# Delta rule on keys and queries as the convolution leaves them: their norms and beta scale rows of the system, the right side and the outputs

## The chip, the cores and the metric

The kernel runs on one core of one Trainium2 chip. The metric is the device time of a run in microseconds (us). The kernel before took 1627.59 us, the median of 3 runs (1624.23 to 1631.69). Beside the timed runs there is one profiled execution, from which every duration below comes.

## The reference, cut to what matters

The program is two layers on 4 sequences ("batches") of 512 tokens with 512 channels. Each layer adds attention times the SiLU of a feed-forward net to its input. The change concerns the attention of the second layer, a gated delta rule with 6 heads of 64:

```
q = silu(causal_conv(x @ Wq.T, conv_q));  k, v likewise
q = q * rsqrt(sum(q*q) + 1e-6);  k = k * rsqrt(sum(k*k) + 1e-6)     # per token and head
beta = sigmoid(x @ Wb.T);  g = -exp(A_log) * softplus(x @ Wa.T + dt_bias)
per token:  S = S * exp(g)
            u = beta * (v - k.S)
            S = S + outer(k, u)
            o = (q * 64**-0.5).S
o = o * rsqrt(mean(o*o) + 1e-5) * o_norm_w * silu(x @ Wg.T);  out = o @ Wo.T
```

The first layer has a softmax attention with 32 heads, and a feed-forward net with Hadamard transforms. The feed-forward net of the second layer multiplies with the signs of its weights.

## The kernel before, in words

Layer 0 fills the first 837 us. One loop over u runs the softmax attention two heads at a time (scores L402, maxima L403, second scores L423, exponentials L425, values L435), and 16 steps behind it the feed-forward net (L316 up and gate, L334 down). In the first batch of it the weights are folded with the Hadamard matrix as they are needed (`mix`, `fold`, loads of `raw`). The same loop also prepares the second layer: `load_weights` and `signs` read each of 32 blocks of the sign weights into a tile `sn` of three buffers, take the sign on ACT (L498) and store it to `sgn_d`. `sn` lies in the pool `zp`, which opens where the pool of the folded weights (`a0`) closes.

Layer 1 works on one batch b after the other, in tiles t of 128 tokens, four a batch.

- *Projections.* `project` (n = 0 to 8: three blocks of 128 channels each of q, k and v) makes one block with the channels on the partitions, convolves it on DVE (L719) and applies SiLU (L723, L724). `to_tokens(b, n, t)` turns three blocks of one tile to tokens on the partitions with three PE transposes (L736), copies them to `z` on ACT (L737), squares them on POOL (L740) and sums the squares per head on DVE (L741). `gate1` makes the output gate and, with its last block, beta and the decays. `norms` turns the sums into 1/norm.
- *Head products.* `scale_heads` on POOL scales k by its norm (L918), makes kb = beta k (L920), scales q (L921), and makes kd and vb (L923, L925). `to_heads` turns kn, kb and qn back to channels on the partitions: nine PE transposes a tile (L933) and three copies on ACT (L935). `tile_decays` makes the decay matrix of a tile (POOL gm L941, PE L943, ACT L945, POOL dT L946). `head_products` multiplies k with kb (A) and with qn (W) (L956), evacuates them times the decays on DVE (L961), and stores the 32x32 diagonal blocks of A to memory.
- *Solve.* `solve_load` reads the 32x32 blocks of the four tiles, one block a partition; 31 `solve_step`s of two DVE operations each (L989, L993) invert them; `solve_store` writes the result, `load_UT` reads it back per tile. In the last batch this is done in two halves of two tiles.
- *Chunk chain.* Per tile `blocks32` to `blocks64b` build the inverse of the 128x128 system from the blocks (products L1020, L1046, evacuated with a factor -1 on ACT, L1023 and L1049), `with_state`, `new_values`, `state` and `outputs` carry the state S through the tiles. `out_norms`, `gated`, `project_out` and `project_out2` end a tile; for all but the last batch they run with the head products of the next.

The calls are put into one list of steps with weights (`add`); while it is emitted, the pieces of the second feed-forward net (`up1` L878, `down1` L891) are strewn in by weight, so that PE has other work. The solve of batch b is strewn among the projections of batch b + 1. A scheduler then orders each engine's instructions by when it thinks that they are ready. All loads and stores after the setup are issued by SP, in order. PSUM gives layer 1's attention three banks (`bank`).

Of the kernel before, what the change touches and what calls it, by code (L numbers as in the profile page):

```python
# [18 lines left out]
P = 128  # L19
# [14 lines left out]
def kernel(ctx: ExitStack, tc: tile.TileContext, i: dict, out: bass.AP):  # L34
# [68 lines left out]
    if True:  # L103
# [383 lines left out]
        def load_weights(n):  # L487
            c, m = n // 2, n % 2
            sg = sns[n] = new(zp[0], [P, DM], F32, "sn", bufs=3)
            if m == 0:  # L490
                nc.sync.dma_start(
                    sg.rearrange("p (k n) -> p k n", k=KC), i["upT"][:, ts(c, P)].rearrange("(k p) n -> p k n", p=P)
                )
            else:
                nc.sync.dma_start(sg, i["downT"][ts(c, P), :])
# [92 lines left out]
    UT_d = new(dram, [NB, TB, NH, 4, 2, 32, 32], F32, "UT_d")  # L588
    gate_d = new(dram, [NB, VC, P, TB, P], F32, "gate_d")


# [45 lines left out]
    for name in ("conv_q", "conv_k", "conv_v"):  # L637
# [15 lines left out]
                            pattern=[[-1, P]], channel_multiplier=1)  # L653

    st = [{} for _ in range(NB)]

    def decays(b):
# [31 lines left out]
    def decay_sums(b):  # L689

        s = st[b]
        small = [P, TB, NH]
        pcum = bank()
        gf = s["g"].rearrange("p t h -> p (t h)")
        for n, m in enumerate((le, gt, ones)):
            nc.tensor.matmul(pcum[:, ts(n, TB * NH)], m, gf, start=True, stop=True)
        ex = s["ex"] = new(ce, [P, 3, TB, NH], F32, "ex", bufs=2)
        nc.scalar.activation(ex.rearrange("p n t h -> p (n t h)"), pcum[:, : 3 * TB * NH], AF.Exp)
        beG = s["beG"] = new(ce, small, F32, "beG", bufs=2)
        nc.vector.tensor_tensor(beG, s["beta"], ex[:, 0], ALU.mult)  # L700
        hb = s["hb"] = new(ce, small, F32, "hb", bufs=2)
        nc.vector.tensor_scalar(hb, s["beta"], 0.5, None, ALU.mult)

        etp = s["etp"] = new(ce, [P, TB, VC], F32, "etp", bufs=2)
        et = ex[:, 2].rearrange("p t (m u) -> p t m u", u=2)
        for u in range(2):
            nc.vector.tensor_copy(etp[64 * u : 64 * u + 64], et[64 * u : 64 * u + 64, :, :, u])

    def project(b, n):

        s = st[b]
        pp = bank()
        for k in range(KC):
            nc.tensor.matmul(pp, wps[b, n][:, k, 0:P], xn1Ts[b][:, k, :], start=(k == 0), stop=(k == KC - 1))  # L714
        w = convs[n // VC][:, n % VC, :]
        yc = new(ce, [P, SEQ], F32, "yc", bufs=4)
        nc.scalar.activation(yc, pp, AF.Copy, scale=w[:, 3:4])
        for d in range(1, 4):
            nc.vector.scalar_tensor_tensor(  # L719
                yc[:, d:], pp[:, : SEQ - d], w[:, 3 - d : 4 - d], yc[:, d:], ALU.mult, ALU.add  # L720
            )
        th = new(ce, [P, SEQ], F32, "cth")
        nc.scalar.activation(th, yc, AF.Tanh, scale=0.5)  # L723
        nc.vector.scalar_tensor_tensor(yc, th, 1.0, yc, ALU.add, ALU.mult)  # L724
        s["yc", n] = yc

    def to_tokens(b, n, t):
        s = st[b]
        if n == 0 and t == 0:
            s["ss"] = new(ce, [P, TB, 2, NH], F32, "ss", bufs=2)  # L730
        if t == 0:
            s["z", n] = new(ce, [P, TB, VD], F32, f"z{n}")
        zt = s["z", n][:, t, :]
        pz = bank()
        for m in range(VC):
            nc.tensor.transpose(pz[:, ts(m, P)], s["yc", VC * n + m][:, ts(t, P)], identf)  # L736
        nc.scalar.copy(zt, pz[:, :VD])  # L737
        if n < 2:
            sq = new(ce, [P, VD], F32, "sq")
            nc.gpsimd.tensor_tensor(sq, zt, zt, ALU.mult)  # L740
            nc.vector.tensor_reduce(s["ss"][:, t, n, :], v6(sq), AX.X, ALU.add)  # L741

# [20 lines left out]
    def norms(b):  # L763
        ss = st[b]["ss"]
        nc.vector.tensor_scalar(ss, ss, 4e-6, None, ALU.add)
        nc.scalar.activation(ss, ss, AF.Sqrt)
        nc.vector.reciprocal(ss, ss)
        nc.vector.tensor_scalar(ss[:, :, 0, :], ss[:, :, 0, :], HD**-0.5, None, ALU.mult)

# [6 lines left out]
    def projections(b, between=()):  # L776
# [16 lines left out]
        for n in range(9):  # L793
# [3 lines left out]
            if n == 1:  # L797
                add(0.3, decay_sums, b)
            if n % 3 == 0 and n:
                for t in range(TB):  # L800
                    add(0.34, to_tokens, b, n // 3 - 1, t)
                    some()
        for m in range(VC - 1):
            prefetch()
            add(3.6, gate1, b, m)
            some()
            if m == 0:
                for t in range(TB):
                    add(0.34, to_tokens, b, 2, t)
                    some()  # L810
                add(0.0, norms, b)
# [10 lines left out]
    cm = ctx.enter_context(tc.tile_pool(name="cm", bufs=1, side="left"))  # L822
    c0 = ctx.enter_context(tc.tile_pool(name="c0", bufs=1, side="left"))
    d0 = ctx.enter_context(tc.tile_pool(name="d0", bufs=2, side="right"))
    dps = ctx.enter_context(tc.tile_pool(name="dps", bufs=1, space=PSUM))
# [88 lines left out]
    def scale_heads(b, t):  # L914
        s = st[b]
        ss = s["ss"]
        qn, kn = s["z", 0][:, t, :], s["z", 1][:, t, :]
        nc.gpsimd.tensor_tensor(v6(kn), v6(kn), bc_in(ss[:, t, 1, :], HD), ALU.mult)  # L918
        kb = s["kb", t] = new(c0, [P, VD], F32, "kb")
        nc.gpsimd.tensor_tensor(v6(kb), v6(kn), bc_in(s["beta"][:, t, :], HD), ALU.mult)  # L920
        nc.gpsimd.tensor_tensor(v6(qn), v6(qn), bc_in(ss[:, t, 0, :], HD), ALU.mult)  # L921
        kd = s["kd", t] = new(c0, [P, VD], F32, "kd", bufs=TB)
        nc.gpsimd.tensor_tensor(v6(kd), v6(kn), bc_in(s["ex"][:, 1, t, :], HD), ALU.mult)  # L923
        vb = s["vb", t] = new(c0, [P, VD], F32, "vb", bufs=TB)
        nc.gpsimd.tensor_tensor(v6(vb), v6(s["z", 2][:, t, :]), bc_in(s["hb"][:, t, :], HD), ALU.mult)  # L925

    def to_heads(b, t):
        s = st[b]
        qn, kn = s["z", 0][:, t, :], s["z", 1][:, t, :]
        for src, tag, n in ((kn, "knT", TB), (s["kb", t], "kbT", 1), (qn, "qnT", TB)):  # L930
            pz = bank()
            for m in range(VC):
                nc.tensor.transpose(pz[:, ts(m, P)], src[:, ts(m, P)], identf)  # L933
            s[tag, t] = new(c0, [P, VC, P], F32, tag, bufs=n)
            nc.scalar.copy(s[tag, t], v3(pz))  # L935

# [11 lines left out]
    def head_products(b, t, right, tag):  # L948
# [4 lines left out]
        for m in range(3):  # L953
            for u in range(2):
                rows = ds(64 * u, 64)
                ins = nc.tensor.matmul(ps[u][:, ts(m, P)], s["knT", t][rows, m, :], s[right, t][rows, m, :],  # L956
                                       start=True, stop=True)
                if m + u > 0:
# [13 lines left out]
    def solve_load(b, t0=0, nt=TB):  # L972
# [3 lines left out]
        Ab = s["Ab"] = new(c0, [P, 32, 32], F32, "Ab")  # L976
        nc.sync.dma_start(Ab[:NBL].rearrange("p r c -> p (r c)"), A_d[b, t0 : t0 + nt].rearrange("t h k r c -> (t h k) (r c)"))
        UT = s["UT"] = new(c0, [P, 2, 32, 32], F32, "UT")
        nc.gpsimd.memset(UT[:, 0], 0.0)
        nc.gpsimd.memset(UT[:, 0].rearrange("p r c -> p (r c)")[:, 0 : 32 * 32 : 33], 1.0)  # L980

    def solve_step(b, j):
# [9 lines left out]
        )  # L992
        nc.vector.tensor_tensor(U[:, 0 : j + 1, j + 1 :], U[:, 0 : j + 1, j + 1 :], x, ALU.subtract)  # L993

# [18 lines left out]
    def blocks32(b, t):  # L1013
# [8 lines left out]
        X = s["X32"] = new(c0, [P, NH, 32], F32, "X32")  # L1022
        nc.scalar.activation(X, px[:, : NH * 32].rearrange("p (h n) -> p h n", h=NH), AF.Copy, scale=-1.0)  # L1023

# [16 lines left out]
    def blocks64(b, t):  # L1041
# [6 lines left out]
        X = s["X64"] = new(c0, [P, NH, 64], F32, "X64")  # L1048
        nc.scalar.activation(X[64:128], v6(px)[64:128], AF.Copy, scale=-1.0)  # L1049

# [10 lines left out]
    def with_state(b, t):  # L1061
# [10 lines left out]
        for m in range(VC):  # L1072
            nc.tensor.matmul(pks[:, ts(m, P)], s["knT", t][:, m, :], S[:, m, :], start=True, stop=True)
        R = s["R"] = new(c0, [P, VD], F32, "R")
# [3 lines left out]
        for m in range(VC):  # L1078
            nc.tensor.matmul(pqs[:, ts(m, P)], s["qnT", t][:, m, :], S[:, m, :], start=True, stop=True)
        tq = s["tq"] = new(c0, [P, VD], F32, "tq")  # L1080
# [41 lines left out]
    def out_norms(b, t=None):  # L1122
        so = st[b]["so"] if t is None else st[b]["so"][:, t]
        nc.vector.tensor_scalar(so, so, 1.0 / HD, EPS, ALU.mult, ALU.add)
        nc.scalar.activation(so, so, AF.Sqrt)
        nc.vector.reciprocal(so, so)

    def gated(b, t):
# [37 lines left out]
    for b in range(NB):  # L1166
# [10 lines left out]
        for t in range(TB):  # L1177
# [5 lines left out]
            for u in range(2):  # L1183
                add(0.7, tile_decays, b, t, u)
                if t >= 2:
                    some(2)
            add(1.1, to_heads, b, t)
            add(0.8, head_products, b, t, "kbT", "A")
            if t >= 2:
                some(3)  # L1190
            if b > 0 and not last:
                add(0.4, project_out, b - 1, t)
            add(0.8, head_products, b, t, "qnT", "W")
            if t >= 2:
# [113 lines left out]
```

## Time and profile before

| what | value |
|---|---|
| median of the runs | 1627.59 us |
| the profiled execution: its time, its span | 1629.15 us, 1627.2 us |
| mean granted TensorE clock | 0.967 |
| layer 0, then layer 1 | 0 to 837 us, 837 to 1627 us |
| head products of batches 0, 1, 2 | 912 to 936.5, 1075 to 1128, 1266 to 1318 us |
| projections of batches 1, 2, 3 | 936.5 to 1011, 1128 to 1200, 1318 to 1392 us |
| critical chain by engine | PE 59%, DVE 22%, DMA 7%, POOL 4%, ACT 4%, issue 3% |

The times of the profile are those of one execution. "Busy" counts an engine's instructions, not how well they use it. Matmuls overlap, so their listed duration is a latency; how long PE is taken by one is read from the starts of two that follow each other. A wait is put down to the operation that came last. The granted clock is 1.00 where TensorE runs at full speed.

### The profile page before, as it was taken

What the parts mean: (1) busy time and instruction counts of PE and PEld (TensorE: products, weight loads), DVE (VectorE), ACT (ScalarE), POOL (GpSimd) and SP (SyncE); (2) the same over time, 40 slices, a digit from 0 to 9 for tenths busy, and PEclk for the clock granted to TensorE, in tenths of its full rate; (3) what the DMA queues carried; (4) which work ended last, traced back from release to release, by engine and by line L of the source; (5) the groups of instructions that cost most, each with busy time, mean ns of one, the idle gap of its engine ahead of it and who ended that gap; (6) DMA issues with size and microseconds to landing.
All of it is one profiled execution on the core that took longest, in us unless ns stands there. A gap on an engine that the chain in (4) does not pass through costs nothing.

```text
span 1627.2 us, 23201 instructions
## 1 busy us (share of the span) xinstructions
PE 1509.9 (93%) x8284; PEld 904.0 (56%) x8284; DVE 1007.8 (62%) x1799; ACT 680.1 (42%) x1007; POOL 419.7 (26%) x424
## 2 busy tenths in 40 slices
PE   6999988999999999999998999989999999999767
PEld 2556432555335543465344666866578666776555
DVE  6899544665556655665437487464946469547754
ACT  4655555666446654565424433132332323222013
POOL 1111100322013210222013713162232713244014
PEclk9999999999999999999998999999999999999779
DMA  7855446665116520363035333344344343333413
GB/s 274 327 192 191 146 151 185 224 219 167 26 45 232 202 75 22 119 225 122 18 89 163 102 105 103 95 143 135 87 128 124 102 125 98 95 98 84 116 45 107
DMA packets 191955, 215.85 MB, mean 133 GB/s; under 512 B 66016, under 2 KB 128864, under 8 KB 190944
## 3 DMA queue, kind: packets, MB, share of 16 engines
q1 hardware_dynamic: 189088, 213.23, 41.5%
q8 instruction: 66, 1.08, 0.3%
q10 hardware_dynamic: 2752, 1.14, 0.3%
q14 instruction: 49, 0.40, 0.1%
HBM read 155.18 MB, written 54.53 MB: 129 GB/s over the span
## 4 chain that ended last, share of the span: by engine, by line
PE 59%; DVE 22%; DMA 7%; POOL 4%; ACT 4%; issue 3%; SPq 1%; POOLq 0%; ACTq 0%; DVEq 0%
PE y L334 13%; PE mm L316 10%; PE ph L878 5%; PE y L891 4%; DVE yc L719 4%; PE sc L402 3%; DVE sx L989 3%; DVE UT L993 3%; PE po L435 2%; DVE nmx L403 2%; PE pu L753 2%; PE mm L243 2%; PE pu L1157 2%; PE pu L1088 1%; PE pu L956 1%
## 5 line engine op out<-in xcount | busy, mean ns | idle before, releaser
L403 DVE TENSOR_REDUCE nmx<-sc 128x2 f32<-128x1024 f32 x256 | 312.2, 1220 | 156.8 <-PE st L423 129.6
L425 ACT ACTIVATE pe<-st 128x1024 f16<-128x1024 f32 x256 | 262.8, 1026 | 145.1 <-PE st L423 143.7
L334 PE MATMUL y<-wdn,hT 128*128 128x512 f32 x512 | 258.7, 626 | 4.7 <-DVE g L338 3.8
L316 PE MATMUL mm<-xr,wc 128*128 128x512 f32 x768 | 209.4, 414 | 0.4 <-DVE th L323 0.4
L327 POOL TENSOR_TENSOR hT<-hT,th 128x512 f32<-128x512 f32 x64 | 83.4, 1303 | 323.3 <-ACT hT L326 249.2
L316 PEld LDWEIGHTS mm<-xr,wc 128*128 128x128 f32 x768 | 138.6, 191 | 49.5 <-issue 21.9
L334 PEld LDWEIGHTS y<-wdn,hT 128*128 128x128 f32 x512 | 87.3, 191 | 93.6 <-issue 85.7
L714 PE MATMUL pu<-xn1T,wp 128*128 128x512 f32 x288 | 129.7, 595 | 0.7 <-DVE yc L719 0.5
L452 POOL TENSOR_TENSOR oT<-os,sm 128x512 f16<-128x512 f32 x32 | 41.4, 1293 | 322.7 <-DMA sm<-rec_d 295.7
L878 PE MATMUL ph<-xsh,sg 128*128 128x512 f32 x256 | 114.4, 447 | 4.3 <-ACT hT L883 2.3
L423 PE MATMUL st<-qm,kT 32*128 32x512 f16 x512 | 102.7, 387 | 9.5 <-ACT pe L425 9.4
L402 PE MATMUL sc<-kT,qT 32*128 32x512 f16 x512 | 102.8, 386 | 8.4 <-DVE nmx L403 8.1
L878 PE MATMUL ph<-xsl,sg 128*128 128x512 f32 x256 | 106.0, 414 | 0.0
L891 PE MATMUL y<-sg,hsh 128*128 128x512 f32 x256 | 90.9, 455 | 4.9 <-DVE hsh L853 3.9
L883 ACT ACTIVATE hT<-ph,upsc 128x512 f32<-128x512 f32 x64 | 44.0, 687 | 111.7 <-PE ph L878 100.9
L714 PEld LDWEIGHTS pu<-xn1T,wp 128*128 128x128 f32 x288 | 53.7, 190 | 57.0 <-issue 53.1
L323 DVE SCALAR_TENSOR_TENSOR th<-th,mm 128x512 f32<-128x512 f32 x64 | 43.6, 682 | 65.5 <-ACT th L322 65.3
L402 PEld LDWEIGHTS <-qT 32*128 32x128 f16 x512 | 26.1, 91 | 101.1 <-issue 94.6
L853 DVE CAST hsh<-hT 128x512 fp32r<-128x512 f32 x64 | 32.4, 507 | 79.3 <-ACT hT L883 79.2
L891 PE MATMUL y<-sg,hsl 128*128 128x512 f32 x256 | 76.5, 412 | 0.0
L316 PE MATMUL mm<-xr,fo 128*128 128x512 f32 x256 | 72.3, 421 | 0.0
L322 ACT ACTIVATE th<-mm,hwg 128x512 f32<-128x512 f32 x64 | 44.0, 688 | 58.9 <-PE mm L316 58.9
(277 smaller groups left out, 2577.9 us busy)
## 6 DMA issues: line engine op xcount, KB each, us to landing
wc<-wS SPq DMA_DIRECT2D x96, 512.0 KB
sg<-sgn_d SPq DMA_DIRECT2D x128, 256.0 KB
wS<-fo SPq DMA_DIRECT2D x16, 1024.0 KB
sm<-rec_d SPq DMA_DIRECT2D x128, 64.0 KB
sgn_d<-sn SPq DMA_DIRECT2D x32, 256.0 KB
raw<-in_w_gateT SPq DMA_DIRECT2D x8, 512.0 KB
hT<-in_w_downT SPq DMA_DIRECT2D x16, 256.0 KB
raw<-in_w_upT SPq DMA_DIRECT2D x8, 512.0 KB
```

Of the source, the lines that this page charges most:

```text
L316: nc.tensor.matmul(pgs[m], wcs[b, c, m][:, h, k, :], xrs[b][:, k, :], start=(k + h == 0), stop=(k == KC - 1 and h == 1))
L327: nc.gpsimd.tensor_tensor(hT, hT, ths[b, c], ALU.mult)
L334: nc.tensor.matmul(ys[t], hTs[b, c][:, ts(t, P)], wdn[:, c, :], start=(c == 0), stop=(c == NI - 1))
L402: nc.tensor.matmul(sc[:, j, :], qTs[n][rows, ts(t, P)], kTs[b, g // 4][rows, :], start=True, stop=True)
L403: nc.vector.tensor_reduce(nmxs[n][:, t, 2 * pr : 2 * pr + 2], sc, AX.X, ALU.max, negate=True)
L423: nc.tensor.matmul(st[:, j, :], kTs[b, g // 4][rows, ts(k, P)], qms[n][rows, :], start=True, stop=True)
L425: nc.scalar.activation(pes[u], st, AF.Exp)
L714: nc.tensor.matmul(pp, wps[b, n][:, k, 0:P], xn1Ts[b][:, k, :], start=(k == 0), stop=(k == KC - 1))
L719: nc.vector.scalar_tensor_tensor(yc[:, d:], pp[:, : SEQ - d], w[:, 3 - d : 4 - d], yc[:, d:], ALU.mult, ALU.add)
L878: ins = nc.tensor.matmul(ph, sgs[b, c, 0][:, ts(k, P)], xss[b][n][:, k, :], start=(k + n == 0), stop=(k == KC - 1 and n == 1))
L891: ins = nc.tensor.matmul(yss[b][t], hss[b, c][n][:, ts(t, P)], sgs[b, c, 1], start=(c + n == 0), stop=(c == NI - 1 and n == 1))
L989: nc.vector.tensor_tensor(x, Ab[:, j, j + 1 :].unsqueeze(1).to_broadcast([NBL, j + 1, r]), U[:, 0 : j + 1, j : j + 1].to_broadcast([NBL, j ...
```

## The change

`scale_heads` no longer scales q and k, kb is gone, and `to_heads` is removed with its transposes. The products, and the products with the state, read the convolution's own output `yc`, which has the channels on the partitions. For that the six blocks of q and k keep a buffer each, in one of two pools by the batch's parity; v's blocks share two. What the norms and beta did is put elsewhere: the rows of the 32x32 blocks are multiplied by c = beta / |k|^2 after their load (DVE; c goes through memory to come to the blocks' partitions), the two evacuations X32 and X64 multiply by -c in place of -1 and so move from ACT to DVE, the right side takes beG and hb with the norms in them, and the output norm takes the q norm in. `to_tokens` is called once per block of channels: four transposes, for q only a square on ACT from PSUM (no z), for k a copy and a square of 512 columns. `norms` computes c and its relatives, transposes -c on PE, and stores it. The sign tiles `sn` move from pool `zp` to pool `b0`.

```diff
-            sg = sns[n] = new(zp[0], [P, DM], F32, "sn", bufs=3)
+            sg = sns[n] = new(b0, [P, DM], F32, "sn", bufs=3)
...
-        yc = new(ce, [P, SEQ], F32, "yc", bufs=4)
+        if n < 2 * VC:
+            yc = new(home[b % 2], [P, SEQ], F32, f"yc{n}")
+        else:
+            yc = new(ce, [P, SEQ], F32, "yv", bufs=2)
...
+    def to_tokens(b, n):
...
+        for t in range(TB):
+            nc.tensor.transpose(pz[:, ts(t, P)], s["yc", n][:, ts(t, P)], identf)
...
+        sq = new(ce, [P, TB, P], F32, "sq")
+        if kind == 0:
+            nc.scalar.activation(sq, pz, AF.Square)
+        else:
+            zt = s["z", 1][:, :, ts(m, P)]
+            nc.scalar.copy(zt, pz)
             nc.gpsimd.tensor_tensor(sq, zt, zt, ALU.mult)
...
     def norms(b):
...
-        nc.vector.tensor_scalar(ss[:, :, 0, :], ss[:, :, 0, :], HD**-0.5, None, ALU.mult)
+        rq = s["rq"] = new(ce, small, F32, "rq", bufs=2)
+        nc.vector.tensor_scalar(rq, ss[:, 0], HD**-0.5, None, ALU.mult)
+        hb = s["hb"] = new(ce, small, F32, "hb", bufs=2)
+        nc.vector.tensor_tensor(hb, s["beta"], ss[:, 1], ALU.mult)
+        c = new(ce, small, F32, "c")
+        nc.vector.tensor_tensor(c, hb, ss[:, 1], ALU.mult)
+        nc.vector.tensor_scalar(hb, hb, 0.5, None, ALU.mult)
+        beG = s["beG"] = new(ce, small, F32, "beG", bufs=2)
+        nc.vector.tensor_tensor(beG, c, s["ex"][:, 0], ALU.mult)
+        ng = s["negc"] = new(ce, small, F32, "negc", bufs=2)
+        for u in range(2):
+            nc.vector.tensor_scalar(
+                ng[:, :, 3 * u : 3 * u + 3], c.rearrange("p t (m u) -> p t u m", u=2)[:, :, u], -1.0, None, ALU.mult
+            )
+        pz = bank()
+        nc.tensor.transpose(pz[: TB * NH, 0:P], ng.rearrange("p t h -> p (t h)"), identf)
+        cr = new(ce, [P, TB, P], F32, "sq")[: TB * NH, 0, :]
+        nc.vector.tensor_copy(cr, pz[: TB * NH, 0:P])
+        nc.sync.dma_start(c_d[b], cr)
...
     def scale_heads(b, t):
-        nc.gpsimd.tensor_tensor(v6(kn), v6(kn), bc_in(ss[:, t, 1, :], HD), ALU.mult)
-        kb = s["kb", t] = new(c0, [P, VD], F32, "kb")
-        nc.gpsimd.tensor_tensor(v6(kb), v6(kn), bc_in(s["beta"][:, t, :], HD), ALU.mult)
-        nc.gpsimd.tensor_tensor(v6(qn), v6(qn), bc_in(ss[:, t, 0, :], HD), ALU.mult)
...
-    def to_heads(b, t):
...
-                ins = nc.tensor.matmul(ps[u][:, ts(m, P)], s["knT", t][rows, m, :], s[right, t][rows, m, :],
-                                       start=True, stop=True)
+                ins = nc.tensor.matmul(ps[u][:, ts(m, P)], s["yc", VC + m][rows, ts(t, P)],
+                                       s["yc", right + m][rows, ts(t, P)], start=True, stop=True)
...
+        cb = new(c0, [P, 32], F32, "cb")
+        nc.sync.dma_start(cb[:NBL], c_d[b, ds(t0 * NH, nt * NH)].rearrange("h (k r) -> (h k) r", r=32))
+        nc.vector.tensor_tensor(Ab[:NBL], Ab[:NBL], bc_mid(cb[:NBL], 32), ALU.mult)
...
-        nc.vector.tensor_tensor(U[:, 0 : j + 1, j + 1 :], U[:, 0 : j + 1, j + 1 :], x, ALU.subtract)
+        nc.vector.tensor_tensor(U[:, 0 : j + 1, j + 1 :], U[:, 0 : j + 1, j + 1 :], x, ALU.add)
...
-        nc.scalar.activation(X, px[:, : NH * 32].rearrange("p (h n) -> p h n", h=NH), AF.Copy, scale=-1.0)
+        nc.vector.tensor_tensor(
+            X, px[:, : NH * 32].rearrange("p (h n) -> p h n", h=NH), bc_in(s["negc"][:, t, :], 32), ALU.mult
+        )
...
-        nc.scalar.activation(X[64:128], v6(px)[64:128], AF.Copy, scale=-1.0)
+        nc.vector.tensor_tensor(X[64:128], v6(px)[64:128], bc_in(s["negc"][64:128, t, :], HD), ALU.mult)
...
     def out_norms(b, t=None):
...
+        for _ in range(2):
+            nc.vector.tensor_tensor(so, so, rq, ALU.mult)
...
+        nc.vector.tensor_tensor(so, so, rq, ALU.mult)
...
-            add(1.1, to_heads, b, t)
-            add(0.8, head_products, b, t, "kbT", "A")
+            add(0.8, head_products, b, t, VC, "A")
```

## The prediction

> **What bounds the kernel now.** I read the page first, then the critical chain, then cut the second half into its stages with the table of stretches. The page's first part says which engine is full:
>
> ```profile
> PE 1509.9 (93%) x8284; PEld 904.0 (56%) x8284; DVE 1007.8 (62%) x1799; ACT 680.1 (42%) x1007; POOL 419.7 (26%) x424
> ```
>
> TensorE is the bound on average, but the stages differ. Six of them (columns: stretch, length, then busy us and count for PE, PEld, DVE, ACT, POOL, then granted clock, DMA share, GB/s):
>
> ```profile
> 912.00:936.50 24.50, 23.36 (x168) 16.05 (x166) 9.99 (x18) 10.45 (x23) 17.19 (x20) 1.00 0.41 116
> 936.50:1011.00 74.50, 70.80 (x304) 47.52 (x304) 62.91 (x155) 25.23 (x45) 21.96 (x23) 0.98 0.38 108
> 1011.00:1075.00 64.00, 64.00 (x626) 53.31 (x625) 33.72 (x61) 13.62 (x24) 15.24 (x16) 1.00 0.36 103
> 1453.50:1482.90 29.40, 24.95 (x147) 17.77 (x145) 10.57 (x19) 9.88 (x21) 22.64 (x26) 0.88 0.21 51
> 1482.90:1524.20 41.30, 33.87 (x134) 21.16 (x132) 35.42 (x79) 6.11 (x12) 10.63 (x10) 0.92 0.50 146
> 1524.20:1570.00 45.80, 25.73 (x238) 20.89 (x239) 29.87 (x81) 4.99 (x9) 3.74 (x5) 0.66 0.20 48
> ```
>
> Row one is the head products of batch 0, row three its chunk chain: PE 95 and 100% busy, so PE work taken out there is time. Row two is the projections of batch 1 with the solve of batch 0 among them; within it DVE is at 9 to 10 tenths from 950 to 1000 us and the critical chain runs through it, so there each DVE microsecond counts too. The last three are batch 3: head products up to its first half solve (POOL 77%), that solve (DVE 86%), and the second half solve, where PE has 20 us idle. PE work taken out of the last two is worth nothing; latency is.
>
> **The change part by part.**
>
> *Transposes removed.* `to_heads` makes nine per tile, 144 in all:
>
> ```profile
> 913.46 0.52 PE L933 MATMUL pu<-identf,z 128*128 128x128 f32 x3
> 913.81 0.49 PE L933 MATMUL pu<-identf,kb 128*128 128x128 f32 x3
> 914.14 0.49 PE L933 MATMUL pu<-identf,z 128*128 128x128 f32 x3
> 914.39 0.48 PE L878 MATMUL ph<-xsl,sg 128*128 128x512 f32 x1
> ```
>
> From the first start to the start of what follows is 0.93 us for nine: 0.11 us a slot when PE is fed (the third column is latency, 286 ns in the group's mean). The Trainium skill, TensorE: Matmul & The Clock Gate, section Part 4: PE-mode transpose, puts one in a kernel at about 275 ns; the 286 ns agree, but by that figure the 108 of batches 0 to 2 would bring 29.7 us (a time near 1599), and by the slot 108 x 0.11 = 11.9 us. I take the slot, because these stretches are back to back. `to_tokens` keeps 144 transposes, regrouped by channel block. **-11.9.** The 48 evacuations on ACT (476 to 494 ns, 23.4 us) and the POOL products for kn, qn and kb (48, 46.8 us by their rows) go as well, as do 16 of 32 squares on POOL; both engines wait most of the time, so by themselves they count nothing. The 12 q copies that become squares on ACT keep the same kind of read.
>
> *What POOL gave to waits.* PE waited for the product evacuation L961, which waits for the decays on POOL:
>
> ```profile
> PE pu L736 <- DVE yc L724: 12.5, 8, 3.3
> PE pu L956 <- DVE A L961: 8.2, 7, 3.7
> ```
>
> Without kb (0.91 us) POOL needs 2 x (0.87 + 1.04) = 3.8 us a tile; batch 0's tiles come every 5.7 us, and 4.8 us after the change, so POOL does not become the bound. The transposes also covered 0.93 us of that latency. Ends: the waits vanish (-8.2), or 12 tiles lose their cover (+11). I take **-1.5**, near nothing.
>
> *Added to projections.* Per batch: five more small DVE operations net (about 0.18 us as L765, so 0.9), one PE transpose (0.11; if it caught DVE late, a table load of 1.28 more) and one 12 KB store plus a load of cb on SP. Both DMAs have slack: batch 0's norms start at 897 us (L765) and its matrices are loaded at 941 (L977); later batches have longer. Six reductions of 128x512 (0.70 by scaling L741's 544 ns) replace eight of 544 ns: nothing. The new product Ab x cb (96 x 1024) has no row; the copy L998 of that size took 1.02 us, the two-input L855 at 128x2048 2.32. I take 1.2 and keep 2.2 for a collision with POOL: solve steps of 0.40 us took 1.37 beside a POOL product. DVE thus gets 2.1 us in each of the stages of batches 1 to 3. Against it: POOL squares fall from eight to three, and in row two four solve steps had stretched by about 0.55 us beside such squares and DVE waited 0.7 us twice for one: -1.8. Net +0.3 each, +0.9 with a range of -2 to +5; batch 0 +0.6, PE's transposes +0.5. **+2.0.**
>
> *A wait at L736.* The 12.5 us above are transposes waiting for the convolution on DVE. Each block is now transposed one projection later, so PE has 3.6 us of work in between. While DVE sets the length, the wait only moves to the next projection's bank. I count nothing; the most is -6.
>
> *Evacuations moved from ACT to DVE.* X32 and X64, 32 in all:
>
> ```profile
> L1049 ACT ACTIVATE X<-pu 64x384 f32<-64x384 f32 x16 | 7.8, 487 | 17.0 <-PE pu L1046 16.8
> L1058 DVE COPY U<-pu 64x384 f32<-64x384 f32 x16 | 8.7, 546 | 12.6 <-PE pu L1056 12.6
> ```
>
> The skill speaks against this (VectorE: DVE Perf Modes, Specifications: ScalarE sits closer to PSUM, VectorE to SBUF). The rows show a difference of 59 ns, so latency hardly changes; what matters is DVE's queue. In batches 0 to 2 DVE is half idle (row three), nothing. In batch 3 tiles 0 and 1 fall between the steps of the second half solve: 2 x (0.36 + 0.55) = 1.8 us of DVE work, with solve steps queued behind an X that waits for PE, and the UT store behind those. At most a round trip per X (4 x 1 us). Value +1.8.
>
> *Batch 3's path.* The first half solve needs A of tile 1: two tiles' transposes (2.0), the kbT and knT copies (1.0) and a kb (0.9) leave the path: -3.9. Added: the first Ab x cb 1.2; Ab's load now queues on SP behind two A stores of tile 2 (0.45 each, 0.9 if A is ready); the second Ab x cb lies under the 4.1 us in which DVE waited for the memset of UT, else 1.2 more. The last tile's norm has three more tiny operations, +0.5. With the 1.8: **+0.5.**
>
> *Sign pass of layer 0.* Moving sn to another pool is not free of effect. The 32 sign loads had to wait for the memory of the folded weights (pool zp takes its place) and ran from 188 to 310 us. The order of instructions now puts the first eleven signs before the 40th exponential, in 140 to 190 us, among the folds; their loads and stores precede the last weight loads and the sm and qT transfers on SP. In 190 to 310 us the passes cost: PE 10.8 us idle, against 1.6 us in 400 to 520, so about 0.3 us a sign. The early stretch has DMA at 0.38 (0.59 later) but DVE at 82% (48%). Ends: -5 (eleven are free there) and +23 (below). I take the same price in both places: **0.**
>
> Sum: -11.9 - 1.5 + 2.0 + 0.5 + 0 = -10.9. The profiled execution took 1629.15 us (span 1627.2); it becomes 1618.2. The median of the runs is 1.6 us lower, hence **1617**.
>
> **The rivals.** (1) *The freed PE time turns into waiting.* For: DVE is at its limit in three stages, POOL holds 77% of batch 3's products, and granted clock falls after gaps (0.66 in the second solve). Against: the two stages that lose the transposes have PE at 95 to 100%. Then half of 11.9 stays, POOL gives nothing and DVE's additions count full (2.1 x 3): -6.0 + 6.3 + 0.5 + 0.5 = about +1, time 1628. (2) *The sign pass collides.* ACT works in order; in the old place it stood 27 us in 18 waits for sn, 1.5 us each. With 0.63 us of work a sign, eleven in a stretch where DVE and PE have no slack cost 11 x 2.1 = 23 us, since exponentials queue behind the sign, and the score banks, the maxima on DVE and the next scores wait for them. -10.9 + 23 = +12: 1640. It is slower by more than 0.5% from 1.7 us a sign on. Against it: three exponential buffers, and the eleven leave the later stretch. (3) *Waits go too*: L736 and L961 lose 10 us together and gaps no longer drop the clock: 1606.
>
> **How the numbers follow.** A measurement of this kernel can tell about 0.5% (8.1 us) from none: the borders are 1619.5 and 1635.7. Forecast 0.47 (1610 to 1623, about three quarters of it under 1619.5), waits go 0.07, freed time lost 0.24, sign collision 0.22. Faster 0.35 + 0.07 = 0.42; same 0.12 + 0.22 = 0.34; slower 0.02 + 0.22 = 0.24. The range 1605 to 1638 leaves out about half of each end case.
>
> **What would show it.** L933 and L935 gone, the heads stretch of batch 0 near 20.5 us and of batches 1 and 2 some 4 us shorter; PE still over 95% there. The projections' stretch unchanged within 1 us, with Ab x cb near 1.2 us. From batch 3's first products to the end the same 174 us within 3. Layer 0 ending within 5 us of 837. I am wrong if layer 0 ends over 8 us later, if PE waits at the products for L961 over 15 us, or if the projections' stretches grow over 3 us each.

## The result, and the profile after

The changed kernel took 1628.7 us, the median of 12 runs (1621.17 to 1633.11), beside 1627.63 us for the kernel before (12 runs, 1622.02 to 1631.69). The ratio is 1.0004 with a 95% interval of 0.9985 to 1.0024: no difference. The forecast was 1617. The profiled execution took 1625.83 us (span 1624.2), 2.9 us under its own median, so where the two profiles differ by a few microseconds I also use the executions of the kernels below that share a stage with them.

The page's first part after the change:

```profile
PE 1488.1 (92%) x8144; PEld 887.3 (55%) x8144; DVE 1022.0 (63%) x1869; ACT 648.7 (40%) x915; POOL 353.1 (22%) x356
```

PE lost 22 us of busy time, ACT 31 and POOL 67, DVE gained 14, and the time stayed. The same six stretches as in the forecast, from the table of stretches of the changed kernel (same columns):

```profile
902.50:922.50 20.00, 17.07 (x122) 10.63 (x120) 9.47 (x18) 5.22 (x10) 12.97 (x14) 1.00 0.34 95
922.50:994.00 71.50, 70.10 (x311) 47.20 (x310) 60.94 (x159) 25.60 (x43) 7.51 (x9) 1.00 0.41 117
994.00:1055.00 61.00, 60.56 (x611) 51.37 (x612) 34.85 (x67) 8.05 (x13) 13.00 (x13) 1.00 0.39 110
1436.00:1469.70 33.70, 23.52 (x131) 15.37 (x129) 13.04 (x26) 7.30 (x12) 23.05 (x25) 0.85 0.16 38
1469.70:1511.40 41.70, 28.32 (x98) 17.11 (x98) 34.69 (x82) 3.76 (x7) 9.08 (x8) 0.81 0.50 144
1511.40:1554.00 42.60, 24.79 (x246) 19.67 (x247) 32.08 (x86) 4.03 (x6) 3.70 (x4) 0.78 0.23 55
```

The head products of batch 0 (row one) went from 24.5 to 20.0 us, close to the 20.5 of the forecast. But PE was busy for 95% of the old row and is busy for 85% of the new one: something else moved too. The heads stretches of batches 1 and 2, which the forecast had some 4 us shorter each, went from 60.4 to 57.7 and from 55.5 to 55.9 us (from the first decay product to the next projection). In row four, the head products of batch 3, POOL's busy time did not fall and the row got 4.3 us longer. Not in these rows is the last tile: from the start of the last group of products L1079 (before, L1056) to the end the kernel before took 23.7 us, the changed one 34.6.

Laid out by stage, in us (executions that share the stage's instructions; their mean in bold):

| stage | before | changed |
|---|---|---|
| layer 0, to the first projection of layer 1 | 841.4, 849.2, 843.2: **844.6** | 834.3 to 843.1 (13, all with `sn` in the new pool): **839.0** |
| layer 1 up to batch 3's head products | 612.2, 610.5, 610.7, 612.3: **611.4** | 600.2 to 606.5 (7): **604.4** |
| batch 3, from there to the end | 173.5, 176.1: **174.8** | **188.2** |

The sum is -5.6 - 7.0 + 13.4 = +0.8 us, which is what the clock of the runs says (0.0004 x 1628 = +0.7). So a gain of 12.6 us arrived and was lost in batch 3. Two places in batch 3 hold the loss. First the last tile, in the timelines of PE (before, then changed) and of DVE (changed). A line has the start, the duration, the engine, the line of the program and the operation; in square brackets stands how long the engine had been idle, and for what:

```profile
1607.13 1.52 PE L1088 MATMUL pu<-R,U 128*128 128x64 f32 x12 [1.14 <-DVE R L1076]
1609.22 1.55 PE L1112 MATMUL pu<-Xv,W 128*128 128x64 f32 x12 [0.57 <-ACT Xv L1091]
...
1611.68 2.84 PE L1157 MATMUL pu<-woT,ogT 128*128 128x512 f32 x6 [0.57 <-ACT ogT L1148]
```

```profile
1591.19 0.88 PE L1102 MATMUL pu<-S,yc 128*128 128x128 f32 x6
1595.18 2.79 PE L1111 MATMUL pu<-R,U 128*128 128x64 f32 x12 [3.11 <-DVE R L1099]
1598.54 2.83 PE L1135 MATMUL pu<-Xv,W 128*128 128x64 f32 x12 [0.57 <-ACT Xv L1114]
...
1602.57 5.49 PE L1185 MATMUL pu<-woT,ogT 128*128 128x512 f32 x6 [0.57 <-ACT ogT L1176]
```

```profile
1591.84 0.55 DVE L1098 TENSOR_TENSOR R<-pu,beG 128x384 f32<-128x384 f32 x1
1592.30 0.68 DVE L1186 SCALAR_TENSOR_TENSOR g1l<-pu,g1l 128x512 f32<-128x512 f32 x1
1592.90 0.85 DVE L935 SCALAR_TENSOR_TENSOR hT<-th,hT 128x512 f32<-128x512 f32 x1
1593.67 1.36 DVE L1099 TENSOR_TENSOR R<-vb,R 128x384 f32<-128x384 f32 x1
...
1608.09 0.69 DVE L1186 SCALAR_TENSOR_TENSOR g1l<-pu,g1l 128x512 f32<-128x512 f32 x1 [4.04 <-PE pu L1185]
1608.70 0.18 DVE L1153 RECIPROCAL so<-so 128x6 f32<-128x6 f32 x1
```

R, the right side of the tile's system, is made by two operations, L1098 and L1099. Between them DVE's queue holds a g1l (the product of an earlier tile's output projection with its feed-forward gate) and a gate product of the feed-forward net, which nobody is in a hurry for; in the kernel before it is one gate product. PE waits 3.11 us (before: 1.14), and the matmuls after the gap take nearly twice their time: 2.79 us for L1111 where it took 1.52 before, 5.49 for L1185 where it took 2.84. Further on the reciprocal of the last output norm stands behind a g1l, which waits 4.04 us for that slow L1185; in the kernel before the reciprocal comes first. The five executions with this order took 34.5 to 35.0 us for the last tile. Of the kernel before there are two with the same last tile, 23.7 and 28.0 us (the second is `b_b0`, below), so the loss here is 6.6 to 10.9 us.

Second, batch 3's head products: PE, then POOL, then SP's queue (SPq: the DMAs that SP issues), all of the changed kernel.

```profile
1455.24 1.65 PE L974 MATMUL pu<-yc,yc 64*128 64x128 f32 x10 [7.46 <-DVE A L979]
```

```profile
1444.55 1.98 POOL L1162 TENSOR_TENSOR O<-O,wrow 128x384 f32<-128x384 f32 x2
1446.49 1.99 POOL L1163 TENSOR_TENSOR og<-O,og 128x384 f32<-128x384 f32 x2
...
1453.60 1.95 POOL L964 TENSOR_TENSOR dT<-dT,le 128x384 f32<-128x384 f32 x2
```

```profile
1455.21 3.62 SPq L985 DMA_DIRECT2D A_d<-A  x8
1458.92 0.37 SPq L896 DMA_DIRECT2D sg<-sgn_d  x1
1462.21 1.69 SPq L985 DMA_DIRECT2D A_d<-A  x2
1464.08 0.31 SPq L995 DMA_DIRECT2D Ab<-A_d  x1
```

A of tile 1 and the load of Ab, in the kernel before and then in the changed one:

```profile
1473.72 1.02 DVE L961 TENSOR_TENSOR A<-pu,dT 128x384 f32<-128x384 f32 x2
1479.23 1.23 SPq L977 DMA_DIRECT2D Ab<-A_d  x1
```

```profile
1454.62 0.56 DVE L979 TENSOR_TENSOR A<-pu,dT 128x384 f32<-128x384 f32 x1 [10.77 <-POOL dT L964]
```

POOL's products of batch 2's gated outputs (L1161 to L1163) stand ahead of the decays of tile 1, so A of tile 1 comes 18.7 us after the start of the stretch, where it came after 20.1 before; the forecast had 3.9 us leave here, and only 1.4 did. Then Ab's load stands behind two stores of tile 2's A, which are not ready until 1462.2: from A's product to Ab's load 9.5 us, before 5.5. Then Ab x cb (1.22 us) and one more product for A: 5.6 us to the first step, before 3.7.

### The profile page after: what moved, and what is told of

Read it like the earlier page. It is cut to its first block, busy times and chain, and to the rows that moved or that the text cites. A ratio compares the mean times of both kernels' runs of the same rounds, so it can differ in the third digit from the quotient of the medians.

```text
span 1624.2 us, 22757 instructions
## 1 busy us (share of the span) xinstructions
PE 1488.1 (92%) x8144; PEld 887.3 (55%) x8144; DVE 1022.0 (63%) x1869; ACT 648.7 (40%) x915; POOL 353.1 (22%) x356
## 3 DMA queue, kind: packets, MB, share of 16 engines
q10 hardware_dynamic: 2752, 1.14, 0.3%
## 4 chain that ended last, share of the span: by engine, by line
PE 59%; DVE 21%; DMA 8%; POOL 4%; issue 3%; ACT 3%; SPq 2%; POOLq 0%; ACTq 0%; DVEq 0%
PE y L334 14%; PE mm L316 10%; PE ph L912 5%; PE y L925 4%; PE sc L402 4%; DVE UT L1014 2%; DVE sx L1010 2%; DVE yc L722 2%; PE po L435 2%; PE pu L1185 2%; DVE nmx L403 2%; PE pu L766 2%; PE mm L243 2%; PE pu L714 1%; PE pu L1111 1%
## 5 line engine op out<-in xcount | busy, mean ns | idle before, releaser
L402 PEld LDWEIGHTS <-qT 32*128 32x128 f16 x512 | 26.2, 91 | 104.3 <-issue 100.1
L925 PEld LDWEIGHTS y<-sg,hsh 128*128 128x128 f32 x256 | 46.4, 193 | 25.0 <-issue 9.1
```

Of the source, the lines that this page charges most:

```text
L402: nc.tensor.matmul(sc[:, j, :], qTs[n][rows, ts(t, P)], kTs[b, g // 4][rows, :], start=True, stop=True)
L925: ins = nc.tensor.matmul(yss[b][t], hss[b, c][n][:, ts(t, P)], sgs[b, c, 1], start=(c + n == 0), stop=(c == NI - 1 and n == 1))
```

## The experiments

Theory: the change's gain is real and is lost in batch 3 by the order in the queues of DVE, POOL and SP. Rivals: (1) the added work on DVE makes batch 3 longer whatever the order; (2) PE's freed time was never worth what the forecast counted. Ratios are to the kernel before, timed beside it on the same chip, with 95% intervals; not all kernels were timed on one chip.

**The last tile.** In `a_tail` two of the gate products and the g1l stand behind tq (the product of q with the state, which follows R), and the g1l of the last two tiles behind the output norm:

```diff
+            if last and t == TB:
+                for q in (2, 3):
+                    add(0.0, behind, "tqi", gate_mlp, b, q)
...
+                        add(2.6, behind, "tqi", project_out2, b, t - 3)
...
+        add(2.6, behind, "soi", project_out2, NB - 1, t)
```

(`behind` issues what it traces on DVE after the named operation; `gate_mlp` is the loop body at the end of `down1`.)

> The changed kernel with only DVE's order in the last tile mended: both halves of R and tq stand ahead of the waiting g1l and of the last two gate products of the feed-forward network, and the last tile's output norm stands ahead of the g1l of project_out2. Theory (queue order: what stands ahead of R and of the reciprocal makes PE idle 3.1 us, the granted clock falls, and the tail's matmuls run at twice their time): from the last b64b to the end about 25 us instead of 34.6, whole kernel 8 to 10 us faster than the changed one (ratio to before about 0.995). Rival 1 (the tail is longer by the work added on DVE, the norms of O, X and the scaling): under 2 us recovered, ratio 1.00. Rival 2 (the clock falls there whatever PE does): R comes earlier by 2 us, but L1111 stays near 2.8 us and the end moves by 2 to 3 us.

It took 0.9962 (0.9947 to 0.9978), and the last tile 25.5 us:

```profile
1602.33 1.52 PE L1114 MATMUL pu<-R,U 128*128 128x64 f32 x12 [0.62 <-DVE R L1102]
1604.42 1.55 PE L1138 MATMUL pu<-Xv,W 128*128 128x64 f32 x12 [0.57 <-ACT Xv L1117]
```

PE waits 0.62 us for R, the same two products take 1.5 us each, and the stretch is 9.1 us shorter with the same work. The theory holds for this place; rival 1 does not. (The ratio moved by 6.8 us of the 9.1, within the intervals.)

`a_fill` leaves DVE's order alone and fills PE's gap:

```diff
+        if b == NB - 1 and t == TB - 1:
+            pf = new(dps, [P, SEQ], F32, "ph")
+            for n in range(6):
+                tc.keep_in_program_order(
+                    nc.tensor.matmul(pf, woT[:, 0, 0:P], woT[:, n % VC, :], start=(n == 0), stop=(n == 5)))
...
```

> The changed kernel with six more matmuls of 128x512 (2.8 us, nobody reads them) in PE's queue in the last tile between the last product with the state and L1111, where PE idled 3.1 us; the queue of DVE stays as it is, so R comes as late as in the changed kernel. Theory (the idle gap lowers the granted clock, and the low clock is most of the tail's loss): L1111 and L1135 back to about 1.5 us each and the first L1185 to 2.8, from the last b64b to the end 28 to 30 us instead of 34.6, ratio 0.997. Rival (R's delay is what counts, or the clock falls by the load of the whole tail): 33 us or more.

0.9989 (0.9975 to 1.0004); the last tile took 30.9 us:

```profile
1603.24 5.32 PE L1109 MATMUL ph<-woT 128*128 128x512 f32 x12
1608.40 1.45 PE L1116 MATMUL pu<-R,U 128*128 128x64 f32 x12
```

The fill took 5.3 us and not 2.8 (I had counted half of its records), so L1116 (the changed kernel's L1111) starts 7.5 us after the last L1079 group's start, where it started 5.6 us after it in the changed kernel. Though 1.9 us later, the tile ends 3.7 us earlier: the low clock that the fill removes is about 5.6 us of its loss. The rest, R's delay and the norm's place, was not tried apart, and the last product with woT takes 4.54 us in both (2.84 before). The ratio alone can't tell it from none.

**Batch 3's first part.** `a_head` wraps the stores of tiles 2 and 3 so that SP issues them after Ab's load, and the gated products so that POOL issues them after the decays of tile 1; `a_head2` has 3 in place of 1:

```diff
+        if b == NB - 1 and t >= 2:
+            with tc.issue_after(s["abi"].ins):
+                store_A(b, t)
...
+    def gated_late(b, t):
+        with tc.issue_after(st[b + 1]["dti", 1].ins):
+            gated(b, t)
```

> The changed kernel with only two queues of batch 3's first part mended: on POOL the gated products of batch 2 stand behind the decays of tile 1, and on SP the load of Ab stands ahead of the stores of A of tile 2. Theory (queue order): from batch 3's first products to the first solve step 26 to 28 us instead of 33.7, and the end comes 5 to 7 us earlier (ratio to before about 0.996). Rival (the stage has a floor in POOL's 22 us and in the latency of the store and load of A; what is taken from one queue comes back in the next): under 2 us. A third outcome is that the first solve starts earlier but PE, which then has its fill of pieces elsewhere, gives it back in the second half.

0.9998 (0.9980 to 1.0015), 31.3 us to the first solve step: neither is what was expected. The wait had only moved to the next tile:

```profile
1468.45 1.65 PE L974 MATMUL pu<-yc,yc 64*128 64x128 f32 x10 [7.50 <-DVE A L979]
```

and Ab x cb, whose load came early, stood on DVE behind that tile's A.

> The changed kernel with the load of Ab ahead of tile 2's stores, as in a_head, and batch 2's gated products on POOL behind the decays of tile 3 instead of tile 1. a_head had moved PE's wait of 7.5 us for the decays from tile 1 to tile 2, and the product Ab x cb stood behind tile 2's A on DVE. Theory (POOL's eleven gated products stand in the way wherever they come before the last decays): from batch 3's first products to the first solve step 22 to 25 us instead of 33.7, no PE wait over 3 us at the head products, and the end 5 to 9 us earlier (ratio 0.996). Rival (the solve isn't what the end waits for; PE's work in batch 3 is): the solve starts 9 us earlier but the end moves by less than 3 us, and PE idles elsewhere.

0.9990 (0.9972 to 1.0008). The first solve step comes after 22.3 us, 11.4 less than in the changed kernel, but the solve behind it takes 47.0 us (41.7), since POOL's products and the output projections of batch 2 now lie in it; from batch 3's start to the end 182.4 us against 188.2. In the profile half of the gain stays, as expected; the timed difference of 2 us is not told from none.

**Both mends, in both kernels.**

> Both mends in the changed kernel. If the two losses are separate, the gains add: 13 to 17 us under the changed kernel, a time near 1614 (ratio to before 0.991). If the clock in the tail is set by how much of the core's work was done before, less than the sum.

> a_head2 and a_tail together. If the parts add: 12 to 16 us under the changed kernel (ratio to before 0.990 to 0.992); if the rival of a_head2 holds, as a_both (0.994).

`a_both` 0.9940 (0.9919 to 0.9960), `a_best` 0.9933 (0.9911 to 0.9954); both gained a little less than was expected (0.991, and 0.990 to 0.992). Batch 3 took 175.5 and 174.9 us, no longer than before the change, with the moved and added DVE work all in it. So rival 1 is out: what was lost in batch 3 was order.

> The same two mends in the kernel before. It has them in a milder form: R waits 1.1 us behind a gate product, decays of tile 0 stand behind nine gated products, and Ab's load already stands ahead of tile 2's stores. Theory: 3 to 5 us faster than before (ratio 0.9975), so that the change is worth 9 to 12 us when both kernels have the same order of queues. Rival 1: nothing, and the change is worth nothing in either order.

> The kernel before with the queue order of a_best (R and the output norm first in the last tile, batch 2's gated products behind the decays of tile 3, Ab's load ahead of tile 2's stores). Set beside a_best (0.9933) it gives the change's worth when neither kernel is held up by those queues. Theory (the change takes about 7 us off before batch 3 and about as much is lost or won in it by order alone): batch 3 from first products to the first solve step 20 to 24 us, ratio 0.997 to 1.000, so the change is worth 6 to 11 us. Rival (the change is worth nothing in any order): 0.9933.

`b_both` 1.0026 (1.0011 to 1.0040): a miss, the same order makes the kernel before no faster; why it is slower stays open (its profile has layer 0 6 to 8 us longer, which the order doesn't touch, and the last tile 2.1 us longer, where one product with woT took 4.54 us instead of 2.84). `b_best` 1.0001 (0.9981 to 1.0021). Beside `a_best` the change is then worth 0.9933 / 1.0001, some 11 us (6 to 16 by the two intervals), in an equal order: the size that was forecast, but not by the forecast's parts, as follows. That the sizes agree is luck.

**The transposes.** `a_tr` puts nine unread transposes per tile into the place of `to_heads` (batches 0 to 2) with its weight of 1.1 in the plan; `a_w` has an empty step of that weight instead:

```diff
+            if not last:
+                add(1.1, dead_transposes, b, t)
             add(0.8, head_products, b, t, VC, "A")
```

> The changed kernel with nine transposes per tile put back where to_heads made them, in batches 0 to 2, with nobody reading them (108 in all), and with their share in the plan that places the feed-forward pieces. Theory of the forecast (0.11 us a slot): heads stretch of batch 0 longer by 4 us, the four stretches up to batch 3's first products by 11.9 us together, ratio to before 1.007. If freed PE time had turned into waiting, half of it, 1.0037; by 275 ns each 29.7 us, 1.018.

> The changed kernel with to_heads' weight of 1.1 given back to the plan in batches 0 to 2 and nothing else: the feed-forward pieces fall where they fell before the change (one piece more in each stretch of head products, one or two fewer in the projections of batches 1 and 2). It is a_tr without its 108 transposes, so the difference to a_tr is their price in a kernel whose pieces stand at the same places. At 0.11 us a slot on full stretches 11.9 us under a_tr (ratio to before about 0.993); if half of it turns into waiting 6 us (0.9965); if the transposes only fill time in which PE would wait, nothing (1.000). Against the changed kernel: if the shift of pieces by the plan has cost it something, as its longer projections of batch 2 suggest (137 us against 132 to 136), up to 6 us faster than it.

`a_tr` 1.0002 (0.9988 to 1.0016), `a_w` 0.9992 (0.9971 to 1.0013): by the ratios the 108 transposes cost 1.6 us, within about 4 us either way, so the 11.9 of the forecast are out and nothing is not. In the profiles layer 1 up to batch 3's products took 607.6 and 605.9 us. (Nobody reads these transposes, so what the old ones cost as links of a chain isn't in this number.) The heads stretch of batch 0 up to the next projection shows how, first with, then without its 36 transposes:

```profile
910.67:937.91 27.24, 26.98 (x200) 20.32 (x199) 11.58 (x25) 5.98 (x13) 13.02 (x14) 1.00 0.39 108
```

```profile
908.08:934.25 26.17, 23.23 (x165) 16.39 (x164) 11.61 (x25) 5.99 (x13) 12.98 (x14) 1.00 0.38 102
```

PE's busy time falls by 3.75 us, which is 0.104 us a transpose, the slot of the forecast. The stretch gets only 1.07 us shorter. PE's waits in the second one (us in all, times, longest) say where the rest is:

```profile
PE pu L961 <- DVE A L979: 2.4, 3, 0.8
PE pu L974 <- DVE A L979: 0.3, 1, 0.3
```

With the transposes there is no such wait. They stood in the time that POOL, ACT and DVE need for a tile's decays and A. Over layer 1 up to batch 3 PE's busy time falls by 9.7 us from `a_tr` to `a_w`, and its idle time rises by 7.9. Rival 2 holds for the transposes.

The plan matters too: without `to_heads`' weight, one feed-forward piece of eight matmuls leaves each stretch of head products, and the stretches from the projections of batches 1 and 2 to their head products get one and two pieces more. The heads stretch of batch 0, measured up to the next projection, was 28.5 us before and 24.4 after: 1.8 of that (26.2 to 24.4) is the piece that moved out, 1.1 (27.2 to 26.2) the transposes, 1.2 the rest. So the 20.0 us near the forecast's 20.5 were luck. The weight also moved the queues: in `a_w`, whose order nobody mended, batch 3's first solve step comes after 29.1 us, as before the change. Still, the timed effect of the weight is nothing (1.0004 and 0.9992, intervals overlapping).

**Layer 0.** `b_b0` is the kernel before with the pool of `sn` changed alone:

```diff
-            sg = sns[n] = new(zp[0], [P, DM], F32, "sn", bufs=3)
+            sg = sns[n] = new(b0, [P, DM], F32, "sn", bufs=3)
```

> The kernel before with only the tiles sn of the sign pass moved to the other pool, as the change moves them: the change's whole effect in layer 0, alone. Forecast: nothing (layer 0 ends within 4 us of 841, the first projection of layer 1). The profile of the changed kernel has layer 0 ending 5.6 us earlier; if that is the signs' doing, ratio 0.9965. If it is the scatter between executions, 1.000 with layer 0 anywhere between 835 and 849, as the other runs of the same layer 0 have it.

0.9975 (0.9959 to 0.9990), 4 us faster: not nothing, and not a collision. Its one profile ends layer 0 at 842.6 us, inside the scatter; the table's means have 5.6 us. So nothing shows a cost of the early signs, as one end of the forecast had it; why the kernel is faster was not looked into.

**Where the freed time waits.** `a_best_w` is `a_best` with the weight of `a_w`.

> a_best with the weight of a_w. If the shift of pieces cost the changed kernel what a_w gives back, this is faster than a_best (0.9933) by as much, to 0.990; if not, the same within 0.15%.

0.9922 (0.9892 to 0.9952), not told from `a_best`. Its largest waits of PE from batch 0's head products to batch 3's, and the worst of them in the timeline:

```profile
PE pu L1189 <- POOL og L1174: 10.1, 2, 5.1
PE pu L977 <- DVE A L982: 3.5, 4, 1.3
PE pu L738 <- DVE yv L727: 3.5, 3, 2.5
PE pu L964 <- DVE A L982: 2.4, 3, 0.8
```

```profile
1075.00 0.90 PE L1189 MATMUL pu<-identf,og 128*128 128x128 f32 x3 [5.11 <-POOL og L1174]
1075.83 1.65 PE L977 MATMUL pu<-yc,yc 64*128 64x128 f32 x12
1077.42 3.58 PE L1200 MATMUL pu<-woT,ogT 128*128 128x512 f32 x6
```

In batches 1 and 2 the first tile's gated output (og) of the batch before is late, and after the gap the products run at 1.65 and 3.58 us (0.93 and 2.84 elsewhere). Before the change this wait was 3.1 us in all, in the changed kernel 7.9; there R, too, kept PE waiting before batch 3, which it did not before the change. In the kernel before, then in the changed one:

```profile
PE pu L1146 <- POOL og L1135: 3.1, 2, 1.6
PE pu L956 <- DVE A L961: 2.2, 4, 1.1
```

```profile
PE pu L1174 <- POOL og L1163: 7.9, 2, 5.2
PE pu L1111 <- DVE R L1099: 5.4, 5, 2.4
PE pu L974 <- DVE A L979: 3.9, 4, 1.7
```

`a_shift` moves the output projection one tile later and puts each tile's gated products behind its decays:

```diff
+            if b > 0 and not last:
+                add(0.0, gated_late, b - 1, t, t)
...
-            if b > 0 and not last:
-                add(0.4, project_out, b - 1, t)
+            if b > 0 and not last and t > 0:
+                add(0.4, project_out, b - 1, t - 1)
```

> a_best_w with the output projection of the batch before moved one tile later in the head products of batches 1 and 2, and its three gated products on POOL behind the decays of the tile they are issued in. In a_best_w PE waits twice for about 5 us for the first tile's gated output, right at the place where the 9 transposes of the changed step used to stand, and its clock falls after it. Theory (the freed PE time went into this wait, the waits for A, and the clock after them): the two waits for og go (10 us), the stretches of batch 1's and 2's heads are 4 to 6 us shorter each, ratio to before 0.985 to 0.988. Rival (another wait on POOL or DVE comes next at the same length): 0.991 to 0.993, as a_best_w.

0.9845 (0.9823 to 0.9867), 1604.02 us: the fastest kernel of this study, 25 us faster than the kernel before. The waits for og are gone from the list, which now begins

```profile
PE pu L977 <- DVE A L982: 6.4, 8, 1.6
PE pu L964 <- DVE A L982: 2.4, 3, 0.8
```

and layer 1 up to batch 3 takes 588.9 us (602.0 in `a_best_w`). Which part of it the shift and which part POOL's order brings was not tried apart.

> a_shift with the 108 dead transposes of a_tr put into the place that holds their weight. Theory (the price of PE work is what PE has no waits to hide it in): with the waits for og gone the transposes cost more here than the 2 us that they cost between a_w and a_tr, 6 to 12 us at 0.11 us a slot, ratio 0.004 to 0.007 above a_shift. Rival (waits for A and the DVE-bound projections hide them in any order): 0 to 3 us, under 0.002 above a_shift.

0.9866 (0.9848 to 0.9885): the transposes cost 3.4 us by the ratios, within about 5 us either way, and 3.5 by the stage. So the wait for og was not what hid most of them: with it gone they still cost a third of their slots in the profile, and the waits for A fall again when they are put in (8.8 to 3.0 us, with 1.7 new for a W). The stage speaks against the theory for this pair (6 to 12 us) and is near its rival; the ratios alone don't decide.

## Why the prediction was wrong, point by point

- *Transposes removed, -11.9.* This step failed. The slot was right (0.104 us measured) and the conclusion wrong: "these stretches are back to back" was read from PE at 95 to 100% busy, but PE was busy because the transposes filled a latency. Worth, by removal with all else equal: 1.6 us in one pair and 3.4 in the other, neither told from nothing, and both clear of 11.9.
- *What POOL gave to waits, -1.5.* This failed for the same reason. I had named the bound (12 tiles lose their cover, +11) and taken "near nothing". Before batch 3 the waits for A went from 2.2 to 6.3 us, for og from 3.1 to 7.9, and for R from nothing to 5.4, which had no term. Over all of layer 1 PE waited 16.6 us for A at the head products (8.2 before), more than the 15 that the forecast had named as a sign of being wrong.
- *A wait at L736, 0 (most -6).* 15.9 us before; L738 waits 10.2 after. At -5.7 the end of the range was right; it may be a large part of the 7.0 us that layer 1 gained before batch 3.
- *Added to projections, +2.0.* Ab x cb took 1.22 us, as taken. The projections of batch 1 took 71.5 us against 74.5: the additions did not show.
- *Evacuations on DVE, +1.8.* From the first 32x32 products of batch 3 to the last group of L1079 78.2 us, before 78.4: nothing.
- *Batch 3's path, +0.5.* This failed, and it is the largest: +13.4 against the mean of the two executions before (8.7 in the last tile, 4.4 up to the first solve step, 0.3 elsewhere). For the last tile I had counted three tiny operations on DVE and not what the scheduler queued between R's two halves and ahead of the reciprocal. For the first part I saw that Ab's load is queued behind two stores and priced it at 0.9 "if A is ready"; A wasn't, and it was 4.0.
- *Sign pass, 0 (ends -5 and +23).* -4 (0.9975).

Of the rivals, the first (freed PE time turns into waiting: half of 11.9 stays, POOL gives nothing; 1628) had both the mechanism and the time, though for its time the loss in batch 3 was needed against gains that it didn't have.

## What to carry to other kernels

An engine at 95 to 100% in a stretch is no proof that work taken off it is time: ask which latency that work covers (here a tile's decays through POOL, ACT and DVE), and whether what comes next on the engine is ready without it. When a change lets a scheduler lay out the queues anew, look up what stands ahead of the critical operations in each queue of the latency-bound stretches, above all in the last tile, where no other work covers a wait; an order that puts them first, with one projection issued a tile later, was worth more here (26 us from the changed kernel to `a_shift`) than the change (11 us in an equal order). And one stage that shrinks as forecast proves little, if work may have been moved out of it.

## What the runs showed of the hardware

In the last tile the low clock cost more than the gap that it followed: about 5.6 us after 3.11. After that wait L1111 took 2.79 us, and 1.45 with the gap filled. Shorter waits can do it too, but don't always: in the kernel before PE waits 1.14 us for R in the last tile and L1112 after it takes 1.55 us; in `b_b0`, with the same instructions there, it went like this, and the last tile took 28.0 us instead of 23.7:

```profile
1606.61 1.52 PE L1088 MATMUL pu<-R,U 128*128 128x64 f32 x12 [1.13 <-DVE R L1076]
1608.70 2.82 PE L1112 MATMUL pu<-Xv,W 128*128 128x64 f32 x12 [0.57 <-ACT Xv L1091]
...
1612.74 5.49 PE L1157 MATMUL pu<-woT,ogT 128*128 128x512 f32 x6 [0.57 <-ACT ogT L1148]
```

The Trainium skill (TensorE: Matmul & The Clock Gate, section Why this matters for your kernels) asks for no PE-idle gaps over about 3 us. The changed kernel's gap agrees with it; `b_b0` shows that 1.13 us and 0.57 us after one another can do as well, and in `a_tail`, with waits of 0.62, 0.57 and 0.57 us, the next product with woT took 4.54 us. The same page (section What's actually happening) has the activity window run freely, so that the moment of a change depends on where in it the first matmul falls. If that holds for gaps as well, the pair before and `b_b0` would fit it; no run here shows it. Between these two profiles the last tile alone makes 4.3 us of scatter.

Beside POOL products, R's subtraction (L1099) took 1.36 us on DVE in the changed kernel. In `a_tail` the same operation took 0.56, and the POOL product that started while it ran took 1.06 (0.83 for the next tile's). These are single instances.
